# v's product of an attention layer by nested seven-product multiplication, with the softmax denominators moved and a new range test

## The chip, the cores and the metric

One NeuronCore of one Trainium2 chip runs the whole program. The metric is the device time of one execution in microseconds. All numbers are float32.

## The reference

Two layers on x of 8 images, 512 channels, 32 x 32 = 1024 positions. The first is attention with 8 heads of 64 channels and a residual, the second a "non-local" block, followed by a normalization over images and positions, channel by channel:

```python
q = conv1x1(x, Wq, bq).reshape(B, h, d, n)      # likewise k, v;  h = 8, d = 64, n = 1024
attn = softmax(einsum('bhdn,bhdm->bhnm', q, k) * d ** -0.5, axis=-1)
out = einsum('bhnm,bhdm->bhdn', attn, v).reshape(B, C, H, W)
x = x + conv1x1(out, Wp, bp)
...
g_x, theta_x, phi_x = (conv1x1(x, w, b).reshape(b, 256, n) for each)
f = einsum('bcn,bdn->bcd', theta_x, phi_x) / n
z = conv1x1(einsum('bcd,bdn->bcn', f, g_x), W_w, W_b) + x
out = (z - mean(z)) * rsqrt(var(z) + 1e-5) * gamma + beta   # over images and positions
```

## The kernel before

`attention_nonlocal_kernel` (L23) runs `unshifted`, which takes exp of the scores without subtracting a maximum. At its end a number comes back that says whether this was safe; if not, `shifted` computes all of it again in the usual way. In the profile of this kernel no instruction of `shifted` stands.

**The stages of an image.** The loop of L859 goes over the images b. For each it issues, in this order: the attention of image b (L436), then q, v and k of image b+1 (L890, L897, L910), then the output projection of image b (`project`, L595), theta and phi (`theta_phi`, L612), and g, f, Wf and z (`nonlocal_`, L679). Image 0's q, k and v come ahead of the loop (L844 to L857). The last image has its own variant; the final normalization is `last_z` (L803).

**Seven products.** A product of two matrices cut into 2 x 2 blocks needs eight block products; `seven` (L263) does it with seven, on sums of blocks that were made beforehand (`weight_sums`, `data_sums`: "t1" to "t4" of x). Each product is accumulated in a PSUM slot of 128 x 1024 (two banks). Four such slots exist, their tags in the list `free`; each stage takes them in that list's order and puts the list in a new order, `next_bank` takes the first and puts it last. A finished product is read out by ScalarE where it is the first to reach its part of the output (`first`), by VectorE where it is added (`add`).

**Nested products.** For q and k (and Wp in images 1 to 6) three (two) of the seven products are replaced by seven smaller ones each, on blocks of 128 x 128: `INNER` (L115) says which, `inner_blocks` and `inner_parts` name the smaller blocks, `keep_inner` (L163) makes the weight sums once and keeps them in DRAM, and `nested` (L245) is a generator that yields after each small product. `STEPS` and `READS` (L241, L242) write by hand after which "unit" of the outer products a small product is issued and an outer slot is read; there are 16 units, and `fills` hangs further work on a unit. v (`values`, L408) isn't nested: it runs all of `SEVEN` with the positions on the output's partitions, so data are the weights that TensorE loads and the moving operand is 256 columns of WvT (L290).

**Attention.** A step makes the scores of 128 keys for 512 queries of two heads (L462, four tiles of 64 x 64 side by side), exp on ScalarE (L465), a running sum `acc` on VectorE (L471), and the product with v (L488). After eight steps `spread` (L503) folds the 128 x 1024 sum to 32 partitions by DMAs that add (`together`, L498: one on SP, three on GpSimd's queue, one behind the other). After every fourth unit a second such fold halves it again into `t[:, 2]` (L522). `all_denominators` (L526) sums the rest over partitions by matmul with `folds8` (`columns`, L431: two tiles of 128 x 64), takes reciprocals (L534), writes them to DRAM (L536), and `rows_of` (L553) spreads them over partitions by four DMAs from SP. `normalize` (L560) gives one function that multiplies o by them, four instructions of 128 x 1024 (L571). Both are hung on products of v: the denominators behind product 1, the multiplications behind product 5 (L897). `r` and the folded sums share one buffer.

**The test.** `heads_of` (L377) takes the peak of |q| and |k| of each channel (L397, four reductions each). `bound_scores` (L421) bounds all scores by the sum over a head of their products (one small matmul, L425), writes one gate per pair of heads, and GpSimd multiplies q by the gate (L429). The minimum of all gates is the result (L968 to L973). `bound_scores` stands within `theta_phi` for images 1 to 7 (L942) and within v for image 0 (L856).

**What sets the order.** Instructions given to `pe`, `dve` or `sp` (L62) keep the order of the program on their engine. The others are placed by a planner that may move them ahead. Every load is a DMA from SP unless said otherwise; weights lie in two buffers, so a load starts when the stage before last has let go of its buffer (`load_w`, L124).

Of the kernel before, what the change touches and what calls it, by code (L numbers as in the profile page):

```python
# [16 lines left out]
P = 128  # L17
HEADS = 8
EPS = 1e-5
BOUND = 60.0  # L20
# [10 lines left out]
def unshifted(ctx: ExitStack, tc: tile.TileContext, a: dict, out: bass.AP):  # L31
# [83 lines left out]
    INNER = {"WqT": (1, 2, 6), "WkT": (1, 2, 6), "WpT": (1, 2)}  # L115
# [26 lines left out]
    def weights(name, sums_done=False):  # L142

        n, w = loaded.pop(0)
        assert n == name
        if name not in kept:
            if not sums_done:
                weight_sums(w, corner[name])
            if name not in ("WqT", "WkT"):
                keep("plain" if name == "WpT" else name, w)  # L150
        return w
# [11 lines left out]
    def keep_inner(name, w):  # L163

        for n in range(len(INNER[name])):
            a11, a12, a22, a21, s2, s3, s4 = inner_blocks(w, name, n)
            for to, l, r, op in ((s3, a11, a21, ALU.subtract), (a21, a21, a22, ALU.add), (s2, a21, a11, ALU.subtract),
                                 (s4, a12, s2, ALU.subtract)):
                nc.vector.tensor_tensor(to, l, r, op)
        wide = len(INNER[name]) * 3 * P  # L170
        kept[name] = dram.tile([P, 14 * w.shape[3] + wide], F32, tag=f"kept_{name}", name=f"kept_{name}")
        nc.sync.dma_start(kept[name][:, :14 * w.shape[3]], w.rearrange("p i k f -> p (i k f)"))
        nc.sync.dma_start(kept[name][:, 14 * w.shape[3]:], rest[name][:, :wide])
# [71 lines left out]
    def nested(name, stage, w, data, tags, first, add):  # L245
# [3 lines left out]
        for n, (q, di, begins) in enumerate(goes_to[i] for i in INNER[stage]):  # L249
# [3 lines left out]
            for _, wi, di, s, reads in SEVEN:  # L253
                ps = pair[s % 2 if s < 2 else 1][:, s // 2, n % 2 * 256:(n % 2 + 1) * 256]
                pe(nc.tensor.matmul(ps, a[wi], d[di], start=s not in begun, stop=True, skip_group_check=True))  # L255
                begun.add(s)
                for to, is_first in reads:
                    c = rows(q).start + int(to[0]) - 1
                    at = cols(q).start + (int(to[1]) - 1) * 256
                    (first if is_first and begins else add)((slice(c, c + 1), slice(at, at + 256)), ps)  # L260
                yield

    def seven(name, w, data, positions_out, first, add, between=None, early=False,  # L263
# [10 lines left out]
        if inner:  # L274
            free[:] = [tags[1], tags[2], tags[3], tags[0]]
            steps = nested(name, inner, w, data, tags[2:], first, add)
# [6 lines left out]
        for n, m in HALVES if three else ((n, None) for n in range(len(products))):  # L283
# [12 lines left out]
            work = [(*part, k) for part in (parts if m is None else parts[m:m + 1]) for k in range(nk)]  # L296
            if by_chunk and what in ("11", "s1t1"):
                work.sort(key=lambda one: one[4])
            for to_ps, at, lhsT, rhs, k in work:
                pe(nc.tensor.matmul(to_ps, lhsT(k), rhs(k), start=(s, at) not in begun, stop=(k == nk - 1),  # L300
                                    skip_group_check=True))
                begun.add((s, at))
                for ahead in (True, False):
# [25 lines left out]
    heads = const.tile([P, P], F32, tag="heads", name="heads")  # L329
    nc.vector.memset(heads, 0.0)  # L330
# [13 lines left out]
    for i in range(WARM):  # L344
        pe(nc.tensor.matmul(ps[:, :P], heads, heads, start=True, stop=True))
# [10 lines left out]
    for i in range(4):  # L356
        nc.vector.memset(folds[i * P // 4:(i + 1) * P // 4, i * D // 4:(i + 1) * D // 4], 1.0)
    folds8 = const.tile([P, D], F32, tag="folds8", name="folds8")
    nc.gpsimd.memset(folds8, 0.0)
    nc.gpsimd.affine_select(out=folds8, in_=folds8, compare_op=ALU.is_gt, fill=1.0, base=1 - P // 8,  # L360
                            pattern=[[-P // 8, 8], [0, D // 8]], channel_multiplier=1)
    nc.gpsimd.affine_select(out=folds8, in_=folds8, compare_op=ALU.is_ge, fill=0.0, base=0,
                            pattern=[[-P // 8, 8], [0, D // 8]], channel_multiplier=1)
    for j in range(2):
        nc.vector.memset(heads[j * D:(j + 1) * D, j * D:(j + 1) * D], 1.0)
    mv = const.tile([P, CC, 2], F32, tag="mv", name="mv")
    gates = const.tile([P, B * NPAIR], F32, tag="gates", name="gates")
# [9 lines left out]
    def heads_of(b, what, w, bias, data, pin=lambda ins: None, later=None, **how):  # L377

        t = mats.tile([P, CC, N], F32, tag=what, name=f"{what}_{b}")
        peak = small.tile([P, CC], F32, tag=f"peak_{what}", name=f"peak_{what}_{b}")  # L380
# [15 lines left out]
        def peak_of(c):  # L396
            ins = nc.vector.tensor_reduce(peak[:, c:c + 1], t[:, c, :], AX.X, ALU.max, apply_absolute_value=True)  # L397
            if b == 0 or later is not None:
                dve(ins)

        for c in range(CC):
            if later is None:
                peak_of(c)
            else:
                later.append(lambda c=c: peak_of(c))
        return t, peak

    def values(b, w, data, between=None):  # L408
        v = mats.tile([P, NB, C], F32, tag="v", name=f"v_{b}")

        def at(q):
            return v[:, (int(q[1]) - 1) * NB // 2:int(q[1]) * NB // 2, (int(q[0]) - 1) * C // 2:int(q[0]) * C // 2]

        def as_v(ps):
            return ps.rearrange("p h (i f) -> p (h i) f", f=C // 2)

        seven(f"pv_{b}", w, data, True, lambda q, ps: nc.scalar.copy(at(q), as_v(ps)),  # L417
              lambda q, ps: dve(nc.vector.tensor_tensor(at(q), at(q), as_v(ps), ALU.add)), between)
        return v

    def bound_scores(b, q, k, peak_q, peak_k):  # L421

        nc.vector.tensor_tensor(peak_q, peak_q, peak_k, ALU.mult)
        ps = next_bank(f"bound_{b}")[:, 0, :]
        pe(nc.tensor.matmul(ps[:, :CC], heads, peak_q, start=True, stop=True))  # L425
        gate = gates[:, b * NPAIR:(b + 1) * NPAIR]
        nc.vector.tensor_scalar(gate, ps[:, :CC], BOUND / SCALE, 1.0, ALU.is_le, ALU.mult)  # L427
        for p in range(NPAIR):
            nc.gpsimd.tensor_scalar(q[:, p, :], q[:, p, :], gate[:, p:p + 1], 1.0, ALU.mult, ALU.mult)  # L429
# [6 lines left out]
    def attention(b, q, k, v, near_end, make_f=None):  # L436
# [66 lines left out]
        def spread(u, pin=lambda ins: None, meanwhile=lambda: None):  # L503
# [18 lines left out]
            if i == 3 and not make_f:  # L522
                two = t[:, g, :].rearrange("(r s) n -> s r n", s=2)
                together(t[g * D:(g + 1) * D, 2, :], [two[0], two[1]])

        def all_denominators(ps):  # L526
# [4 lines left out]
            t, ps = t[:, 2, :], ps[:, 0, :]  # L531
            columns(ps, folds8, lambda j: t[:, j * 512:(j + 1) * 512])
            ri = t[:, :512]
            nc.vector.reciprocal(ri, ps)  # L534
            d = dram2.tile([16, 512], F32, tag="den", name=f"den_d_{b}")
            nc.sync.dma_start(d, ri.rearrange("(a s) n -> a s n", a=16)[:, 0, :])  # L536
            d = d.rearrange("(j g i) n -> g j (i n)", j=2, g=2)
            return d[0], d[1]

        def denominators(g, ps):  # L540
# [8 lines left out]
            d = dram2.tile([8, 512], F32, tag=f"den{g}", name=f"den_d_{b}_{g}")  # L549
            nc.sync.dma_start(d, ri.rearrange("(a s) n -> a s n", a=8)[:, 0, :])  # L550
            return d.rearrange("(j i) n -> j (i n)", j=2)

        def rows_of(g, d):  # L553
# [3 lines left out]
            for j in range(2):  # L557
                sp(nc.sync.dma_start(rows[g][j * D:(j + 1) * D, :], d[j].partition_broadcast(D)))

        def normalize(d):  # L560
# [6 lines left out]
            def products():  # L567
                for g in range(2):
                    for h in range(NH):
                        at = o["o"][:, 2 * g:2 * g + 2, h * 512:(h + 1) * 512]  # L570
                        dve(nc.vector.tensor_tensor(at, at, r[:, 4 * g + h:4 * g + 4:2, :], ALU.mult))  # L571

            return products
# [179 lines left out]
    late, z = {}, {}  # L753
# [90 lines left out]
    q, peak_q = heads_of(0, "q", weights("WqT", True), bq, data, early=True, by_chunk=True)  # L844
    keep_inner("WqT", w_first)
    load_w(nc.sync)
# [5 lines left out]
    w = weights("WkT")  # L852
    k, peak_k = heads_of(0, "k", w, bk, data)
    keep_inner("WkT", w)
    load_w(nc.sync)
    v = values(0, weights("WvT"), data, {3: lambda: bound_scores(0, q, k, peak_q, peak_k)})  # L856
    load_w(nc.sync)  # L857
    held = {}
    for b in range(B):  # L859
# [23 lines left out]
        if not last:  # L883
            later, of_22, of_t4 = [], [], []
# [4 lines left out]
                     8: lambda: (of_22[0](), of_22[1]()), 9: lambda: (of_22[2](), of_22[3]())}  # L889
            q, peak_q = heads_of(b + 1, "q", weights("WqT"), bq, nxt["data"], dve, inner="WqT",  # L890
                                 later=later, fills=fills)
            load_w(nc.sync)

            def norm():
                nxt["products"] = normalize(denominators(next_bank(f"den_{b}")))

            v = values(b + 1, weights("WvT"), nxt["data"], {1: norm, 2: lambda: [one() for one in later], 5: lambda: nxt["products"]()})  # L897
# [7 lines left out]
            else:  # L905
                w_p = loaded[1][1]
                for unit, which in ((12, (3, 4)), (14, (5, 6))):
                    fills[unit] = lambda which=which: weight_sums(w_p, corner["WpT"], which, dve)
            later_k = []
            k, peak_k = heads_of(b + 1, "k", weights("WkT"), bk, nxt["data"], later=later_k, inner="WkT",  # L910
                                 fills=fills)
# [3 lines left out]
        else:  # L915
# [4 lines left out]
            normalize(nxt["d"])()  # L920
# [16 lines left out]
        elif b > B - LATE and b != B - 2:  # L937
# [3 lines left out]
                       {5: lambda: b < B - 2 and of_theta.append(f_sums(b, tps[0], 0)), 1: lambda: [one() for one in later_k[:2]], 2: lambda: [one() for one in later_k[2:]],  # L941
                        4: lambda: bound_scores(b + 1, q, k, peak_q, peak_k)})  # L942
# [20 lines left out]

    last_z()


    good = const.tile([P, 1], F32, tag="good", name="good")
    nc.vector.tensor_reduce(good, gates, AX.X, ALU.min)  # L968
# [215 lines left out]
```

## Time and profile before

| what | us |
|---|---|
| median of 3 runs | 2145.33 |
| lowest and highest run | 2145.25, 2148.92 |
| span of the profiled execution, first to last instruction | 2143.6 |
| median less that span | 1.7 |

The profiled execution has no other time of its own than the span; the 1.7 us stand for what lies around the instructions. The granted TensorE clock was 0.996 of full speed in the mean.

Where the span goes, for the attention of image 1 and what follows it, by the first TensorE instruction of each stage on the timeline:

| stage | from | to | us |
|---|---|---|---|
| attention of image 1 | 343.48 | 453.51 | 110.03 |
| q of image 2 | 453.51 | 476.42 | 22.91 |
| v of image 2, with the denominators of image 1 | 476.42 | 501.80 | 25.38 |
| k of image 2 | 501.80 | 524.60 | 22.80 |
| projection of image 1 | 524.60 | 547.80 | 23.20 |
| theta and phi | 547.80 | 572.20 | 24.40 |

How to read the lines: a matmul of float32 stands as two PE rows. The duration of a row holds the way through the array, so two rows overlap; what a row costs TensorE is the distance between starts. A row of the timeline joins like instructions: start, length, engine, line, operation, output and inputs, "128*128" the part of the array, the shape of the moving operand and the count.

### The profile page before, as it was taken

How to read it: one execution, taken by the hardware profiler on the slowest of the kernel's cores; microseconds unless marked ns; L12 is line 12 of the kernel's file. 1: busy time of each engine (PE TensorE's matmuls, PEld its weight loads, DVE VectorE, ACT ScalarE, POOL GpSimd, SP SyncE). 2: the span in 40 equal slices, each digit the busy share in tenths (PEclk: the TensorE clock that was granted, in tenths of full speed). 3: DMA queues.
4: the chain of work that ended last, by engine and by line, in shares of the span. 5: the costliest groups of instructions: out<-in, count | busy, mean ns of one | idle time of the engine just before them, and what ended most of it. 6: DMA issues, size and time to landing. Idle time of an engine off the chain costs nothing.

```text
span 2143.6 us, 30444 instructions
## 1 busy us (share of the span) xinstructions
PE 2119.6 (99%) x12654; PEld 1123.3 (52%) x12654; DVE 1448.4 (68%) x1795; ACT 742.8 (35%) x848; POOL 193.2 (9%) x242
## 2 busy tenths in 40 slices
PE   9999999999999999999999999999999999999996
PEld 4534664356733567335673366633666347743462
DVE  6467667667676676766667667676675676756736
ACT  1464104641046310463105621066212652056106
POOL 0111000110001100011001100011000110011000
PEclk9999999999999999999999999999999999999998
DMA  6433443334143331433323342233434235122758
GB/s 242 137 46 58 136 166 127 49 71 129 73 131 49 79 116 73 133 50 83 109 102 109 48 100 99 97 107 50 108 132 161 42 45 139 52 60 39 227 197 341
DMA packets 53969, 231.05 MB, mean 108 GB/s; under 512 B 9792, under 2 KB 16192, under 8 KB 46272
## 3 DMA queue, kind: packets, MB, share of 16 engines
q1 hardware_dynamic: 42144, 199.26, 27.5%
q0 software_dynamic: 10192, 28.46, 11.0%
q8 instruction: 101, 1.65, 0.3%
q10 hardware_dynamic: 1488, 1.32, 0.2%
q14 instruction: 44, 0.36, 0.1%
HBM read 141.84 MB, written 46.27 MB: 88 GB/s over the span
## 4 chain that ended last, share of the span: by engine, by line
PE 96%; ACT 1%; DVE 1%; DMA 1%; issue 0%; SPq 0%; ACTq 0%; DVEq 0%
PE ps L462 21%; PE po L488 21%; PE pv L300 9%; PE ptp L300 9%; PE pp L300 7%; PE pk L300 6%; PE pq L300 5%; PE pg L300 4%; PE pk_in_s L255 3%; PE pq_in_s L255 3%; PE pz L300 2%; PE pf L658 2%; PE pp_in_s L255 2%; PE pwf L713 1%; ACT z L830 1%; PE pf L674 1%
## 5 line engine op out<-in xcount | busy, mean ns | idle before, releaser
L465 ACT ACTIVATE e<-ps 128x1024 f32<-128x1024 f32 x512 | 522.6, 1024 | 431.1 <-PE ps L462 425.6
L471 DVE TENSOR_TENSOR acc<-acc,e 128x1024 f32<-128x1024 f32 x384 | 470.0, 1224 | 143.7 <-ACT e L465 140.3
L462 PE MATMUL ps<-q,k 64*64 64x512 f32 x4096 | 529.4, 589 | 0.0
L488 PE MATMUL po<-e,v 64*64 64x512 f32 x4096 | 528.7, 589 | 0.0
L488 PEld LDWEIGHTS po<-e,v 64*64 64x64 f32 x4096 | 156.6, 133 | 282.9 <-issue 275.4
L462 PEld LDWEIGHTS ps<-q,k 64*64 64x64 f32 x4096 | 155.5, 133 | 283.8 <-issue 274.8
L501 POOL DMA_DIRECT2D fold<-acc x189 | 147.1, 779 | 978.9 <-DMA fold<-acc 576.6
L701 ACT ACTIVATE g<-pg,gb 128x512 f32<-128x512 f32 x31 | 21.3, 687 | 475.4 <-PE pg L300 475.3
L469 DVE TENSOR_TENSOR acc<-e,e 128x1024 f32<-128x1024 f32 x64 | 78.3, 1224 | 136.6 <-ACT e L465 136.6
L300 PE MATMUL pv<-w_WvT,t_x 128*128 128x256 f32 x512 | 116.4, 381 | 0.0
L300 PE MATMUL ptp<-w_tp,t_x 128*128 128x256 f32 x512 | 114.4, 379 | 0.0
L417 ACT COPY v<-pv 128x1024 f32<-128x1024 f32 x32 | 32.4, 1012 | 213.9 <-PE pv L300 213.9
L300 PEld LDWEIGHTS pv<-w_WvT,t_x 128*128 128x128 f32 x512 | 96.6, 190 | 18.5 <-issue 5.7
L300 PEld LDWEIGHTS ptp<-w_tp,t_x 128*128 128x128 f32 x512 | 97.3, 190 | 13.2
L300 PE MATMUL pq<-t_x,w_WqT 128*128 128x512 f32 x200 | 100.1, 592 | 0.8 <-DVE t_x L842 0.8
L300 PE MATMUL pp<-t_o,w_WpT 128*128 128x512 f32 x208 | 100.8, 592 | 0.0
L300 PE MATMUL pk<-t_x,w_WkT 128*128 128x512 f32 x200 | 100.0, 592 | 0.0
L429 POOL TENSOR_SCALAR q<-q,gates 128x1024 f32<-128x1024 f32 x32 | 35.1, 1109 | 718.4 <-DVE gates L427 718.4
L300 PE MATMUL ptp<-w_tp,x 128*128 128x256 f32 x384 | 87.4, 381 | 0.0
L300 PE MATMUL pv<-w_WvT,x 128*128 128x256 f32 x384 | 86.8, 379 | 0.0
L324 DVE TENSOR_TENSOR q<-q,pq_in_s 128x256 f32<-128x256 f32 x119 | 48.6, 420 | 51.1 <-PE pq_in_s L255 38.4
L324 DVE TENSOR_TENSOR k<-k,pk_in_s 128x256 f32<-128x256 f32 x119 | 47.9, 420 | 48.6 <-PE pk_in_s L255 36.0
(195 smaller groups left out, 2348.6 us busy)
## 6 DMA issues: line engine op xcount, KB each, us to landing
fold<-acc POOLq DMA_DIRECT2D x189, 128.0 KB, 3.1
w_WqT<-kept_WqT SPq DMA_DIRECT2D x7, 2368.0 KB, 8.8
w_WkT<-kept_WkT SPq DMA_DIRECT2D x7, 2368.0 KB, 8.8
r<-den_d SPq DMA_DIRECT2D x32, 512.0 KB, 6.9
x<-in_x_dram SPq DMA_DIRECT2D x30, 512.0 KB, 5.7
w_WpT<-kept_WpT SPq DMA_DIRECT2D x6, 2176.0 KB, 8.3
w_WvT<-kept_WvT SPq DMA_DIRECT2D x7, 1792.0 KB, 7.2
w_tp<-kept_tp SPq DMA_DIRECT2D x7, 1792.0 KB, 7.3
```

The lines of the kernel that those rows point to most:

```text
L255: pe(nc.tensor.matmul(ps, a[wi], d[di], start=s not in begun, stop=True, skip_group_check=True))
L300: pe(nc.tensor.matmul(to_ps, lhsT(k), rhs(k), start=(s, at) not in begun, stop=(k == nk - 1), skip_group_check=True))
L324: pin(nc.vector.tensor_tensor(at, at, ps if len(ps.shape) == 3 else ps.unsqueeze(1), ALU.add))
L417: seven(f"pv_{b}", w, data, True, lambda q, ps: nc.scalar.copy(at(q), as_v(ps)), lambda q, ps: dve(nc.vector.tensor_tensor(at(q), at(q), a ...
L429: nc.gpsimd.tensor_scalar(q[:, p, :], q[:, p, :], gate[:, p:p + 1], 1.0, ALU.mult, ALU.mult)
L462: pe(nc.tensor.matmul(ps[c * P // 2:(c + 1) * P // 2, j, :], k[r, p, keys], q[r, p, h * 512:(h + 1) * 512], start=True, stop=True, skip_gr ...
L465: nc.scalar.activation(e, ps, AF.Exp, scale=SCALE)
L469: nc.vector.tensor_tensor(accs[u], es[u, 0], e, ALU.add)
L471: ins = nc.vector.tensor_tensor(accs[u], accs[u], e, ALU.add)
L488: pe(nc.tensor.matmul(ps[j * D:(j + 1) * D, r, :], v[keys, m, (2 * p + j) * D:(2 * p + j + 1) * D], e[keys, j, :], start=(m == 0), stop=(m ...
L501: nc.gpsimd.dma_start(to, part_of, accum_op=ALU.add)
L658: pe(nc.tensor.matmul(to, theta[l][:, i, :], phi[r][:, i, :], start=(i == 0), stop=(i == NB // 2 - 1), skip_group_check=True))
```

## The change

It is made in `unshifted` only.

- **v is nested like q and k.** `INNER` gets WvT with the same three products; `nested` and `seven` learn the case `positions_out`, in which a small product is two matmuls of 128 moving columns; v's outer products are the four of `FOUR`. Between q and v the list `free` is put in another order by hand.
- **The denominators come at unit 14 of q**, into the slot `free[0]`. The second fold is gone; the matmul uses four tiles of 32 columns (`folds4`), and the reciprocals are of 128 x 256. The order of the reciprocals in DRAM is another, and `rows_of` and `product` address them accordingly. The reciprocal is pinned.
- **The multiplications are hung one by one** on units 10 to 13 of v.
- **The test is another**: peaks, `bound_scores` and gates are gone; the reciprocals of all denominators are loaded back at the end (`own`, nine DMAs) and each has to lie between 1e-20 and 1e20.
- **Around image 0**: q's and k's additions and WkT's sums are pinned, `keep_inner("WqT")` moves behind WkT's sums and is pinned, `keep_inner("WvT")` stands behind v.

```diff
-    INNER = {"WqT": (1, 2, 6), "WkT": (1, 2, 6), "WpT": (1, 2)}
+    INNER = {"WqT": (1, 2, 6), "WkT": (1, 2, 6), "WvT": (1, 2, 6), "WpT": (1, 2)}
...
-                nc.vector.tensor_tensor(to, l, r, op)
+                dve(nc.vector.tensor_tensor(to, l, r, op))
...
-                pe(nc.tensor.matmul(ps, a[wi], d[di], start=s not in begun, stop=True, skip_group_check=True))
+                if positions_out:
+                    ps = ps.rearrange("p (i f) -> p i f", f=P)
+                    for i in range(2):
+                        pe(nc.tensor.matmul(ps[:, i, :], d[di][:, i * P:(i + 1) * P], a[wi], start=s not in begun and not i,
+                                            stop=True, skip_group_check=True))
+                else:
+                    pe(nc.tensor.matmul(ps, a[wi], d[di], start=s not in begun, stop=True, skip_group_check=True))
                 begun.add(s)
                 for to, is_first in reads:
+                    if positions_out:
+                        (first if is_first and begins else add)((q, int(to[0]) - 1, int(to[1]) - 1), ps)
+                        continue
...
-            work = [(*part, k) for part in (parts if m is None else parts[m:m + 1]) for k in range(nk)]
+            each = len(parts) // 2
+            work = [(*part, k) for part in (parts if m is None else parts[m * each:(m + 1) * each]) for k in range(nk)]
...
+                if three and positions_out and not i % 2:
+                    continue
...
-        def peak_of(c):
-            ins = nc.vector.tensor_reduce(peak[:, c:c + 1], t[:, c, :], AX.X, ALU.max, apply_absolute_value=True)
...
-    def bound_scores(b, q, k, peak_q, peak_k):
...
-            if i == 3 and not make_f:
-                two = t[:, g, :].rearrange("(r s) n -> s r n", s=2)
-                together(t[g * D:(g + 1) * D, 2, :], [two[0], two[1]])
...
-            t, ps = t[:, 2, :], ps[:, 0, :]
-            columns(ps, folds8, lambda j: t[:, j * 512:(j + 1) * 512])
-            ri = t[:, :512]
-            nc.vector.reciprocal(ri, ps)
...
+            ps, of = ps[:, 0, :256], P // 4
+            for g in range(2):
+                for i in range(4):
+                    pe(nc.tensor.matmul(ps[i * of:(i + 1) * of, :], folds4[:, g * of:(g + 1) * of],
+                                        t[:, g, i * 256:(i + 1) * 256], start=(g == 0), stop=(g == 1),
+                                        skip_group_check=True))
+            ri = t[:, 2, :256]
+            dve(nc.vector.reciprocal(ri, ps))
+            d = dram.tile([of, 256], F32, tag=f"den{b}", name=f"den_d_{b}")
+            nc.sync.dma_start(d, ri.rearrange("(x s) n -> x s n", s=4)[:, 0, :])
+            own.append((dens[:, b * 64:(b + 1) * 64], d.rearrange("x (y n) -> (x y) n", y=4)))
+            return d.rearrange("(j h g i) m -> g j h i m", j=2, h=2, g=2)
...
-            def products():
-                for g in range(2):
-                    for h in range(NH):
-                        at = o["o"][:, 2 * g:2 * g + 2, h * 512:(h + 1) * 512]
-                        dve(nc.vector.tensor_tensor(at, at, r[:, 4 * g + h:4 * g + 4:2, :], ALU.mult))
-
-            return products
+            def product(g, h):
+                at = o["o"][:, 2 * g:2 * g + 2, h * 512:(h + 1) * 512]
+                of = r[:, 4 * g + h:4 * g + 4:2, :]
+                if not make_f:
+                    of = r[:, 4 * g:4 * g + 4, :].rearrange("q (k a) (c m) -> q (a c) k m", k=2, c=2)[:, h::2]
+                    at = at.rearrange("q p (k m) -> q p k m", k=2)
+                dve(nc.vector.tensor_tensor(at, at, of, ALU.mult))
+
+            return [lambda g=g, h=h: product(g, h) for g in range(2) for h in range(NH)]
...
-    q, peak_q = heads_of(0, "q", weights("WqT", True), bq, data, early=True, by_chunk=True)
-    keep_inner("WqT", w_first)
-    load_w(nc.sync)
+    q = heads_of(0, "q", weights("WqT", True), bq, data, dve, early=True, by_chunk=True)
...
-    w = weights("WkT")
-    k, peak_k = heads_of(0, "k", w, bk, data)
+    w = weights("WkT", pin=dve)
+    keep_inner("WqT", w_first)
+    load_w(nc.sync)
+    k = heads_of(0, "k", w, bk, data, dve)
     keep_inner("WkT", w)
     load_w(nc.sync)
-    v = values(0, weights("WvT"), data, {3: lambda: bound_scores(0, q, k, peak_q, peak_k)})
+    w = weights("WvT")
+    v = values(0, w, data)
+    keep_inner("WvT", w)
...
+                     14: lambda: nxt.update(products=normalize(denominators(bank(free[0], f"den_{b}"))))}
+            q = heads_of(b + 1, "q", weights("WqT"), bq, nxt["data"], dve, inner="WqT", fills=fills)
             load_w(nc.sync)
...
-            v = values(b + 1, weights("WvT"), nxt["data"], {1: norm, 2: lambda: [one() for one in later], 5: lambda: nxt["products"]()})
+            free[:] = [free[2], free[1], free[0], free[3]]
+            v = values(b + 1, weights("WvT"), nxt["data"], inner="WvT",
+                       fills={unit: lambda i=i: nxt["products"][i]() for i, unit in enumerate((10, 11, 12, 13))})
...
-                        4: lambda: bound_scores(b + 1, q, k, peak_q, peak_k)})
+                       {5: lambda: b < B - 2 and of_theta.append(f_sums(b, tps[0], 0))})
...
+    for to, d in own:
+        nc.sync.dma_start(to, d)
     last_z()
...
-    nc.vector.tensor_reduce(good, gates, AX.X, ALU.min)
+    nc.vector.tensor_scalar(sane, dens, 1.0 / SANE, 1.0, ALU.is_ge, ALU.mult)
+    nc.vector.scalar_tensor_tensor(sane, dens, SANE, sane, ALU.is_le, ALU.mult)
+    nc.vector.tensor_reduce(good, sane, AX.X, ALU.min)
```

## The prediction

> **What bounds the kernel now.** I read the page first: which engine is busy, and what the chain that ended last is made of.
>
> ```profile
> PE 2119.6 (99%) x12654; PEld 1123.3 (52%) x12654; DVE 1448.4 (68%) x1795; ACT 742.8 (35%) x848; POOL 193.2 (9%) x242
> PE 96%; ACT 1%; DVE 1%; DMA 1%; issue 0%; SPq 0%; ACTq 0%; DVEq 0%
> ```
>
> TensorE (PE) is never idle for long, and the chain is TensorE nearly throughout. A busy PE can still be a slow PE, so next I read the timeline of one steady image row by row, to see whether rows follow each other at a constant pace.
>
> ```profile
> 317.81 1.05 PE L658 MATMUL pf<-tp 128*128 128x128 f32 x8
> 318.70 1.06 PE L658 MATMUL pf<-s_phi,s_theta 128*128 128x128 f32 x8
> ...
> 324.06 1.88 PE L300 MATMUL pg<-x,w_WgT 128*128 128x512 f32 x4
> ...
> 476.42 3.62 PE L300 MATMUL pv<-w_WvT,x 128*128 128x256 f32 x16
> 479.87 3.62 PE L300 MATMUL pv<-w_WvT,t_x 128*128 128x256 f32 x16
> 483.42 1.08 PE L434 MATMUL den<-fold,folds 128*64 128x512 f32 x4
> 484.43 3.72 PE L300 MATMUL pv<-w_WvT,t_x 128*128 128x256 f32 x16
> ...
> 501.80 3.60 PE L300 MATMUL pk<-x,w_WkT 128*128 128x512 f32 x8
> 505.23 0.59 PE L255 MATMUL pk_in_s<-x,w_WkT 128*128 128x256 f32 x2
> ```
>
> From start to start: 8 rows of 512 columns take 505.23 - 501.80 = 3.43 us, 0.429 each; 16 rows of 256 take 479.87 - 476.42 = 3.45, 0.216 each; the 56 rows of 128 of the product f take 324.06 - 317.81 = 6.25, 0.1116 each. A row costs its columns and little else. k of image 2 is 32 rows of 512 and 42 of 256: 13.73 + 9.07 = 22.80 us, exactly what the stage takes (501.80 to 524.60). So the nested stages run without a gap although VectorE (DVE) reads every small product behind them. The time of this kernel is its count of columns plus a few stalls, and I price the change that way.
>
> **The nested v, seven images.** Before: 7 products of 8 matmuls, 112 rows of 256, 112 x 0.2159 = 24.18 us. After: four outer products, 64 rows of 256, 13.82 us; and 3 x 7 small products of two matmuls, 84 rows of 128, 84 x 0.1116 = 9.37 us. Together 23.19: 0.99 us less an image, 7.0 us in seven. The price of a 128-column row decides: it breaks even at (24.18 - 13.82) / 84 = 0.1234 us. The nearest row is f's, with the same 128 x 128 weights, loaded anew for every matmul. Below it lies half a 256-column row, 0.108 (2.2 us more gain); above, the mean 0.190 of a weight load in the rows of PEld, which would be the pace if loads were not hidden (46 us lost). I take 0.1116, since f shows them hidden.
>
> The Trainium skill speaks against this part: "TensorE: Matmul & The Clock Gate", section "Back-to-back issue gap", says that a stream of pairs of weight load and matmul sustains about 81 ns at 128 columns and 131 ns at 512, so that a short matmul is dear per column. By that ratio a row of 128 would be an estimated 0.429 x 81 / 131 = 0.265 us, and the nested v would lose 83 us in all. This case's rows stand at 0.1116 against 0.429, a ratio of 0.26 where the page has 0.62; I go by the rows.
>
> Does VectorE keep up in v? Of the 21 small reads four go to ScalarE, 17 to VectorE at 0.42; with three outer reads and four multiplications of 1.22 that is 15.7 us in 23.2. In q's window before it is 15.62 busy in 22.91, without a gap on TensorE. If this cover were gone, a late read stops TensorE at the next small product that accumulates into the same slot; that is the second rival. The reductions of the peaks (eight an image, 1.16 to 1.22 each) and GpSimd's gating (35 us in all) go, but hid behind TensorE: worth nothing.
>
> **The denominators.** They cost TensorE four rows of 512 in two tiles, two at a time, plus the way in and out of that tiling: from where the next v row was due (483.11 + 0.22 = 483.33) to 484.43, and 0.1 more behind, 1.2 us. After: 16 rows of 256 in four tiles of 32 columns, that is four rounds of 0.216 = 0.86 if four run side by side as the 64 x 64 tiles of attention do (eight rows of 512 in 0.86), plus the same way in and out (0.34): 1.2 again. No row shows 128 x 32 tiles. Ends: 0.86 (gain 0.34 an image) and one after the other, 16 x 0.216 + 0.34 = 3.8 (loss 2.6). I take 1.2, by the attention row. The skill's page "TensorEngine Tiling (Array Packing)", section "Available Configurations", lists 128 x 32 as four tiles; no run here shows it, and by it the sum is the one I take.
>
> They now come some 8 us earlier than before, so what they wait for matters:
>
> ```profile
> 468.36 0.51 SPq L499 DMA_DIRECT2D fold<-fold  x1
> 487.93 0.50 SPq L536 DMA_DIRECT2D den_d<-fold  x1
> 489.85 2.40 SPq L558 DMA_DIRECT2D r<-den_d  x4
> 473.37 1.22 DVE L324 TENSOR_TENSOR q<-q,pq 128x1024 f32<-128x1024 f32 x1
> 476.96 2.34 DVE L324 TENSOR_TENSOR q<-q,pq 128x1024 f32<-128x1024 f32 x2
> 484.55 3.36 DVE L534 RECIPROCAL fold<-den 128x512 f32<-128x512 f32 x1 [5.25 <-PE den L434]
> 502.35 2.36 DVE L571 TENSOR_TENSOR o<-o,r 128x1024 f32<-128x1024 f32 x2 [0.31 <-DMA r<-den_d]
> ```
>
> The first fold is complete when SP issues the second, at 468.36. Behind unit 14's small product the new matmul is due at 475.13: 6.8 us to spare. The second fold, whose last part GpSimd issued at 472.84 and which lands 3.1 later by the median, would have been too late; it is gone. Its slot is that of the outer product whose last read is the VectorE row at 473.37, done at 474.6: 0.5 to spare. The reciprocal, at 3.36 us for 512 columns, is 1.7 for 256, pinned ahead of q's last three reads: it waits until 476.4 and ends at 478.1, and those reads end at 480.8 instead of 479.3. v starts at 477.5 and needs the slot they read only in its unit 4, at 482. Then SP: store, spreading from 480.0, the fourth DMA issued at 481.8, landed by its median of 6.9 us at 488.7 (longest 11.5: 493.3). Unit 10 of v, where the first multiplication is due, ends at 477.5 + 11 x 0.864 + 14 x 0.446 = 493.2. k's weights, which SP issued at 476.61, wait behind the spreading until 482.4 and land about 9 us later; k starts at 500.7. All covered; cost nothing.
>
> **The bound's matmul goes, eight times.** theta and phi are 112 rows, 24.18 us, and the stage takes 572.20 - 547.80 = 24.40: 0.22. For image 0 v takes 78.30 - 53.80 = 24.50: 0.32. Sum 7 x 0.22 + 0.32 = 1.8 us.
>
> **The start.** TensorE loses 1.0 us at 15.96, waiting for a sum of x:
>
> ```profile
> 13.79 0.29 DVE L169 TENSOR_TENSOR w_WkT<-w_WkT 128x128 f32<-128x128 f32 x1 [1.86 <-DMA w_WkT<-in_WkT_dram]
> 14.00 0.69 DVE L842 TENSOR_TENSOR w_WqT<-w_WqT 128x512 f32<-128x512 f32 x1
> 14.60 1.22 DVE L842 TENSOR_TENSOR t_x<-x,t_x 128x1024 f32<-128x1024 f32 x1
> 15.96 3.67 PE L300 MATMUL pq<-t_x,w_WqT 128*128 128x512 f32 x8 [0.84 <-DVE t_x L842]
> ```
>
> A sum of `keep_inner` that nobody needs yet stands ahead of it on VectorE and waits 1.86 us for WkT. Pinned behind q's additions it can't. The last piece of x, issued at 7.97, lands by the median of 5.7 at 13.7, so the sum could start 0.9 earlier. Nothing later in image 0 shows a gap that would eat it. I take 0.9, between 0 and 1.0.
>
> **Around image 0 and at the end.** `keep_inner("WvT")` adds 12 sums of 0.29 to the start of attention, where VectorE is busy 77.78 of 110.03 us: hidden, 3.5 us if not. The test adds nine loads on an idle SP and three VectorE instructions of 128 x 512, about 0.5 + 0.7 + 0.6. The old minimum ran as soon as its inputs were there (1869), not at the end, so I take 0; in the last VectorE chain it would be 1.8.
>
> **Sum.** -7.0 - 1.8 - 0.9 = -9.7 us on the span of 2143.6: 2133.9. The median run is 1.7 above that span; I keep this distance: 2145.33 - 9.7 = **2135.6 us**.
>
> **Rivals.**
> *Slower: the four 32-column tiles run one after the other.* Then 7 x 2.6 = 18.2 comes back: 2153.8. It decides from 2.6 us a call (1.2 + 9.7 / 7). For it: no such row in the trace, and each pair of rows of one matmul meets the same tile. Against: 64-column and 64 x 64 tiles do overlap.
> *About the same: VectorE is late in v.* In units 10 to 13 it gets four multiplications, one outer addition and seven small reads. Back to back, rows follow at 1.13 (two rows in 2.34) and 0.34 (by the same overlap of 0.085): 5 x 1.13 + 7 x 0.34 = 8.0 us, where TensorE takes 4 x 0.864 + 7 x 0.446 = 6.6. It ends 1.4 behind, and a small product two further on in the same slot comes 1.3 later. If 1 us of it reaches TensorE in each image, 7.0 comes back: 2142.6. For it: k, the model, has only two such operations in a row; and a multiplication already waited 0.31 for `r`. Against: VectorE enters unit 10 without arrears, and `r` has 4.5 us to spare by the median, none by the longest.
> *The change doesn't do what it says: rows of 128 are dear here*, because each is aimed at another piece of PSUM, where f stays on one for four matmuls, and the loads show. At 0.190 a row, 84 x 0.078 x 7 = 46 comes back: 2181.6. Against: q's and k's small products change their piece as often and cost their columns.
>
> **Chances.** Forecast 0.76; late VectorE 0.13; serial tiles 0.08; dear rows 0.03. 0.2% of the time is 4.3 us, about what a measurement of this kernel tells from no change: faster 0.77 (a mild lateness of VectorE counts here), same 0.12, slower 0.11. The forecast's own range is 2133 to 2139 (cheaper rows and denominators below; start, test and WvT's sums above). The range reaches to the late VectorE: 2133 to 2143.5, and leaves out the two slower cases.
>
> **What would show it.** v's stage at 23.2 us without a gap, its rows of 128 at 0.11; a den group in q at unit 14 that takes 1.2 in four rounds, with no wait ahead of it; theta and phi at 24.18; the wait at 15.96 gone; a multiplication that doesn't wait for `r`. Wrong would be: gaps at v's small products, den rows that start 0.2 apart, or a VectorE test in the last 20 us.

## The result and the profile after

The changed kernel takes 2152.64 us in the median of 7 runs (2151.52 to 2154.09), the kernel before 2145.59 in 7 (2145.25 to 2148.92). The ratio is 1.0031, 95% interval 1.0021 to 1.0042: slower by 7.05 us. That lies above the range of the prediction. The profiled execution of the changed kernel has a span of 2152.2 us, 8.6 more than before. It is the slowest of the seven (2154.09, 1.45 above the median), so its trace shows a little more loss than the median has; the last section shows a loss of 1.45 us that one execution may have and another not.

The page of the changed kernel, its engines and its chain of waits:

```profile
PE 2116.7 (98%) x12974; PEld 1124.5 (52%) x12974; DVE 1412.1 (66%) x1855; ACT 745.9 (35%) x869; POOL 144.9 (7%) x193
PE 89%; DMA 6%; DVE 2%; ACT 1%; issue 1%; SPq 1%; DVEq 0%; ACTq 0%
```

TensorE has fewer us of work than before (2119.6) in a longer span, and its share of the chain fell from 96% to 89%: DMA took 6% of it, where it had 1%. So the question is not what TensorE does more slowly, but which transfer it waits for. The chain itself answers; it is read in order of time around the end of q and v of image 2 (start, length, what):

```profile
476.03 1.04 PE den L523 x16
...
477.10 1.76 DVE fold L527
...
478.97 9.17 DMA den_d<-fold
...
490.26 10.48 DMA r<-den_d
...
501.98 1.22 DVE v L420
...
503.77 0.71 PE pv_in_s L258 x4
```

The denominators (`den`, 16 rows of TensorE), the reciprocal (`fold`, L527), its store to DRAM (`den_d`), the spreading of it over partitions (`r`), a row of VectorE and then the last small product of v: the path of the reciprocals, which the prediction held to be covered, sets the end. Its first transfer, 32 KB, takes 9.17 us. SP's own queue at that time shows what stands ahead of it:

```profile
478.55 0.33 SPq L134 DMA_DIRECT2D w_WkT<-kept_WkT  x1
478.97 0.49 SPq L529 DMA_DIRECT2D den_d<-fold  x1
488.28 2.59 SPq L555 DMA_DIRECT2D r<-den_d  x4
```

k's weights (2368 KB) were issued 0.4 us ahead of the store. The spreading needs the store landed, so it begins at 488.28, 9.3 us behind the store. This image is the worst: in the other six the distance is 8.2 to 8.4. In the kernel before it was 1.9 us (487.93 to 489.85), since there the weights were issued 11 us ahead of the store:

```profile
476.61 0.33 SPq L134 DMA_DIRECT2D w_WkT<-kept_WkT  x1
487.93 0.50 SPq L536 DMA_DIRECT2D den_d<-fold  x1
```

VectorE and then TensorE at the end of v in the changed kernel:

```profile
493.86 0.42 DVE L420 TENSOR_TENSOR v<-v,pv_in_s 128x256 f32<-128x256 f32 x1 [0.89 <-PE pv_in_s L258]
496.12 1.23 DVE L572 TENSOR_TENSOR o<-o,r 128x1024 f32<-128x1024 f32 x1 [1.84 <-DMA r<-den_d]
497.26 0.75 DVE L420 TENSOR_TENSOR v<-v,pv_in_s 128x256 f32<-128x256 f32 x2
...
500.84 1.23 DVE L572 TENSOR_TENSOR o<-o,r 128x1024 f32<-128x1024 f32 x1 [0.84 <-DMA r<-den_d]
501.98 1.21 DVE L420 TENSOR_TENSOR v<-v,pv 128x1024 f32<-128x1024 f32 x1
503.30 0.42 DVE L420 TENSOR_TENSOR v<-v,pv_in_s 128x256 f32<-128x256 f32 x1
```

```profile
495.86 1.03 PE L310 MATMUL pv<-w_WvT,t_x 128*128 128x256 f32 x4
497.73 0.71 PE L258 MATMUL pv_in_s<-w_WvT,i_x 128*128 128x128 f32 x4 [0.84 <-DVE v L420]
...
501.39 1.03 PE L310 MATMUL pv<-w_WvT,t_x 128*128 128x256 f32 x4
503.77 0.71 PE L258 MATMUL pv_in_s<-w_WvT,i_x 128*128 128x128 f32 x4 [1.36 <-DVE v L420]
504.32 3.60 PE L310 MATMUL pk<-x,w_WkT 128*128 128x512 f32 x8
```

In these rows VectorE keeps to the program's order. Its first multiplication of `o` waits 1.84 us for `r`, the third 0.84, and v's small reads (`v<-v,pv_in_s`, the additions that empty a small product's slot) queue behind them. TensorE's next small product accumulates into a slot that such a read has yet to empty. After the four rows at 495.86 it was due at 496.73 and starts at 497.73; after those at 501.39 it was due at 502.25 and starts at 503.77. That is 2.5 us of the 2.77 by which v of this image (25.96 us) exceeds the 23.19 that its columns alone cost.

The spans by stage, before and after, from the starts of their first matmuls, account for the 8.6 us:

| stages | before | after | difference |
|---|---|---|---|
| q, denominators and v, images 1 to 7 | 339.2 | 347.9 | +8.7 |
| k, images 1 to 7 | 159.9 | 162.1 | +2.2 |
| theta and phi with the bound | 195.1 | 193.5 | -1.6 |
| v of image 0 | 24.5 | 24.3 | -0.2 |
| start up to k of image 0 | 29.8 | 29.9 | +0.1 |
| the rest (projection and tail) | | | -0.6 |

The nested v itself takes 178.0 us in the seven images; its columns are 7 x 23.19 = 162.3. So 15.7 us of v are stops, and they are what turned a gain into a loss. Of the +2.2 in k, 1.45 stand in image 5 alone, where the granted clock fell for a while (last section).

### The profile page after: what moved, and what is told of

Its sections match the earlier page's. It is cut to its first block, busy times and chain, and to the rows that moved or that the text cites. A ratio compares the mean times of both kernels' runs of the same rounds, so it can differ in the third digit from the quotient of the medians.

```text
span 2152.2 us, 31116 instructions
## 1 busy us (share of the span) xinstructions
PE 2116.7 (98%) x12974; PEld 1124.5 (52%) x12974; DVE 1412.1 (66%) x1855; ACT 745.9 (35%) x869; POOL 144.9 (7%) x193
## 4 chain that ended last, share of the span: by engine, by line
PE 89%; DMA 6%; DVE 2%; ACT 1%; issue 1%; SPq 1%; DVEq 0%; ACTq 0%
PE ps L454 20%; PE po L480 20%; PE ptp L310 9%; PE pp L310 7%; PE pk L310 5%; PE pq L310 5%; PE pg L310 4%; DMA r<-den_d 3%; PE pk_in_s L261 3%; PE pq_in_s L261 3%; DMA den_d<-fold 3%; PE pz L310 2%; PE pf L659 2%; PE pp_in_s L261 2%; PE pwf L714 1%; PE pv L310 1%
## 5 line engine op out<-in xcount | busy, mean ns | idle before, releaser
L310 PE MATMUL pv<-w_WvT,t_x 128*128 128x256 f32 x400 | 100.7, 380 | 0.0
L420 DVE TENSOR_TENSOR v<-v,pv_in_s 128x256 f32<-128x256 f32 x119 | 48.5, 420 | 62.5 <-PE pv_in_s L258 48.5
L310 PEld LDWEIGHTS ptp<-w_tp,x 128*128 128x128 f32 x384 | 73.0, 190 | 13.3 <-issue 3.8
L310 PEld LDWEIGHTS pv<-w_WvT,t_x 128*128 128x128 f32 x400 | 69.6, 191 | 6.0
L400 ACT ACTIVATE k<-pk,bk 128x512 f32<-128x512 f32 x50 | 31.6, 683 | 114.8 <-PE pk L310 114.8
```

The costliest lines, as they stand in the source:

```text
L400: nc.scalar.activation(t[:, c, cols(q)], ps[:, m, :], AF.Identity, bias=bias[:, c:c + 1])
```

## The experiments

The theory: the order on SP's queue. The store stands behind the weights, `r` comes late, and VectorE's queue carries the lateness to TensorE. The main rival: VectorE simply has too much to do at the end of v, whatever `r` does. Another: the nested v is dear in itself. The first four kernels ran on one chip beside a kernel before of 2145.98 us (29 runs), the last three on another beside one of 2145.81 (15 runs). All ratios are to the kernel before.

**weights_behind.** The load of k's weights is pinned on SP (given to `sp`), so that it keeps its place in the program: behind the store and the four spreading DMAs.

```diff
-    def load_w(dma):
+    def load_w(dma, pin=lambda ins: None):
...
             ins = dma.dma_start(t[:, :of.shape[1]], of)
+            pin(ins)
...
             q = heads_of(b + 1, "q", weights("WqT"), bq, nxt["data"], dve, inner="WqT", fills=fills)
-            load_w(nc.sync)
+            load_w(nc.sync, sp)
```

> The changed kernel with one DMA moved: the load of k's weights is pinned on SP behind the four DMAs that spread the reciprocals. Theory A (the 2.4 MB load stands ahead of the store of the reciprocals on SP; r comes some 7 us late, VectorE waits for it with v's small reads behind, TensorE stops): the store lands in about 2 us, no multiplication waits for r, v takes 23.2 us in each image instead of 24.6 to 26.4, 2136 us in all (2145.6 - 9.2). Theory B (VectorE has too much to do in units 10 to 13 of v even with r in time): v stays at 24.2 or more, 2143 us. Theory C (small products of 128 columns are slow by themselves): no change, 2152 us.

2139.18 us, ratio 0.9971 (0.996 to 0.9982). v takes 23.58 in each of the seven images, k 22.86 from image 2 on. SP's queue, and then VectorE:

```profile
476.68 0.49 SPq L530 DMA_DIRECT2D den_d<-fold  x1
478.57 2.59 SPq L556 DMA_DIRECT2D r<-den_d  x4
481.26 0.58 SPq L134 DMA_DIRECT2D w_WkT<-kept_WkT  x1
```

```profile
495.40 0.94 DVE L421 TENSOR_TENSOR v<-v,pv_in_s 128x256 f32<-128x256 f32 x2
496.25 1.22 DVE L573 TENSOR_TENSOR o<-o,r 128x1024 f32<-128x1024 f32 x1
497.39 1.21 DVE L421 TENSOR_TENSOR v<-v,pv 128x1024 f32<-128x1024 f32 x1
498.71 0.42 DVE L421 TENSOR_TENSOR v<-v,pv_in_s 128x256 f32<-128x256 f32 x1
499.04 1.22 DVE L573 TENSOR_TENSOR o<-o,r 128x1024 f32<-128x1024 f32 x1
```

The spreading begins 1.9 us after the store's issue, no multiplication of this image waits for `r`, and k doesn't wait for its weights, though they are issued 4.6 us behind the store and land 16 us after that. This one edit takes the ratio from 1.0031 to 0.9971, some 13 us. That the weights go ahead of the store is the cause of the loss. It is still 3 us more than theory A expected (2136). What stays is a small remainder of the rival: VectorE's rows follow one another without a wait and still the small read at 498.71 is late. TensorE loses 0.39 us an image by it (23.58 against 23.19).

**other_queue.** The weights stay where they are, and the store and the spreading are issued from GpSimd's queue instead of SP's.

```diff
-            nc.sync.dma_start(d, ri.rearrange("(x s) n -> x s n", s=4)[:, 0, :])
+            nc.gpsimd.dma_start(d, ri.rearrange("(x s) n -> x s n", s=4)[:, 0, :])
...
-                    sp(nc.sync.dma_start(to, d[j].rearrange("h i m -> h (i m)").partition_broadcast(D)))
+                    sp(nc.gpsimd.dma_start(to, d[j].rearrange("h i m -> h (i m)").partition_broadcast(D)))
```

> The changed kernel, with the store of the reciprocals and their spreading issued by GpSimd's queue; k's weights are still loaded from SP just ahead. If the store is late because it stands in SP's own line behind the weights: it lands in about 2 to 3 us as the folds do from that queue (3.1 by the median), r is in time, about 2137 us. If it is late because the DMA engines are full with the weights whatever the queue: it lands after 7 to 9 us as before, 2151 to 2153 us. Theory C: 2152 us either way.

2142.42 us, ratio 0.9983 (0.9974 to 0.9993). v takes 23.58 to 25.20. GpSimd's queue:

```profile
480.13 0.58 POOL L529 DMA_DIRECT2D den_d<-fold  x1 [12.02 <-DVE q L336]
487.11 2.34 POOL L555 DMA_DIRECT2D r<-den_d  x4 [6.40 <-PE pv_in_s L258]
```

Neither of the two expected times came; the result lies between them. The spreading begins 7.0 us behind the store in this image and 6.9 to 7.3 in images 3 to 7, where the changed kernel has 8.2 to 8.4: another queue takes off some 1.2 us, not the 6.4 that would bring it to 1.9. GpSimd's wait is put down to a matmul, but what ends it is the store: SP's own load of the same reciprocals, which waits for it too, starts at 486.42, 6.3 us after the store's issue, and GpSimd's first spreading DMA follows 0.7 later. The weights that SP had issued at 479.52 are still under way. So what the store stands behind is mostly the transfer, and not SP's queue alone. The Trainium skill says why in "DMA: Bandwidth & Descriptors", section "Issuing engines are not separate DMA queues": DMAs from all issuing engines run on the same 16 DMA engines and interleave. The 6.9 to 7.3 here agree with it.

**products_in_k.** The order on SP is as in the changed kernel, but nothing in v waits for `r`: the four multiplications are hung on units 1 to 4 of k.

```diff
-            v = values(b + 1, weights("WvT"), nxt["data"], inner="WvT",
-                       fills={unit: lambda i=i: nxt["products"][i]() for i, unit in enumerate((10, 11, 12, 13))})
+            v = values(b + 1, weights("WvT"), nxt["data"], inner="WvT")
...
+            fills.update({unit: lambda i=i: nxt["products"][i]() for i, unit in enumerate((1, 2, 3, 4))})
```

> The changed kernel with the four multiplications hung on units 1 to 4 of k instead of units 10 to 13 of v; the weights are still ahead of the store. Theory A: r is as late as before, but nobody in v waits for it; v 23.2 us, k 22.8 to 23.5 (r lands about 4 us ahead of k), 2136 to 2139 us. Theory B: v 23.2 as well, but k, which has other fills, loses what v gains: 2139 to 2143. Theory C: v stays at 25, 2152 us.

2144.53 us, ratio 0.9993 (0.9984 to 1.0003): no difference to the kernel before. The stages v and k of image 2, one line each (stretch, length, then busy time and count of PE, PEld, DVE, ACT, POOL, the granted clock, DMA's share, GB/s), and k's stop:

```profile
476.56:499.75 23.19, 23.19 (x150) 21.55 (x149) 10.94 (x21) 4.52 (x7) 0.00 (x0) 1.00 0.71 199
499.75:523.72 23.97, 23.58 (x77) 13.65 (x76) 19.91 (x32) 5.64 (x10) 0.00 (x0) 1.00 0.25 93
```

```profile
506.75 0.70 PE L261 MATMUL pk_in_s<-x,w_WkT 128*128 128x256 f32 x2 [0.39 <-DVE k L336]
```

The nested v without the multiplications takes 23.19, PE busy all of it: the third theory is out, the products themselves cost what was forecast. But the time is above all that theories A and B expected (2136 to 2143), because k now takes 23.97 instead of 22.86: its own small reads queue behind the multiplications. The multiplications aren't free at these units of k either.

**v_not_nested.** Everything of the change but the nested v: seven products as before, the multiplications behind product 5.

```diff
-            v = values(b + 1, weights("WvT"), nxt["data"], inner="WvT",
-                       fills={unit: lambda i=i: nxt["products"][i]() for i, unit in enumerate((10, 11, 12, 13))})
+            v = values(b + 1, weights("WvT"), nxt["data"], between={5: lambda: [one() for one in nxt["products"]]})
```

> The changed kernel with v by seven products as before the change, the multiplications behind product 5; the denominators stay at unit 14 of q, the weights ahead of the store, the new test stays. Theory A: r lands about when product 5 ends, and few reads stand behind it; v 24.2 us without a stop; what is left of the change is the bound's matmuls, 2143 to 2144 us, so nesting v with the late r costs 9 us where it should have brought 7. Theory B: the same. Theory C: the same, so this run measures nesting alone and tells only how much of the loss is v's.

2143.76 us, ratio 0.9987 (0.9978 to 0.9997). SP's queue and the stage v:

```profile
477.15 0.33 SPq L134 DMA_DIRECT2D w_WkT<-kept_WkT  x1
477.57 0.49 SPq L529 DMA_DIRECT2D den_d<-fold  x1
485.88 2.59 SPq L555 DMA_DIRECT2D r<-den_d  x4
```

```profile
476.95:501.12 24.17, 24.17 (x113) 21.29 (x112) 8.72 (x9) 3.04 (x3) 0.00 (x0) 1.00 0.68 190
```

The spreading begins 8.3 us behind the store here too, and it costs nothing: v takes exactly its 24.17, PE busy throughout. The four multiplications follow product 5's read, at 499.01 on VectorE, and don't wait: by then `r` has landed. That is 22.1 us into v; in the changed kernel the first was due at 494.3, 15.9 us into v, and waited. VectorE is busy for only 8.72 us of this stage. So the loss is made by two parts of the change together, the late store and the early use of `r` in the nested v. Neither the order on SP nor the nested v has such a price alone.

**half_ahead.** A dose: the first half of k's weights goes ahead of the store as before, the second half behind the spreading.

```diff
+            if ahead:
+                at = of.shape[1] // ahead
+                dma.dma_start(t[:, :at], of[:, :at])
+                with tc.issue_after(spread_last[-1]):
+                    dma.dma_start(t[:, at:of.shape[1]], of[:, at:])
+                return
...
-            load_w(nc.sync)
+            load_w(nc.sync, 2)
```

> The changed kernel with k's weights loaded in two halves: the first still ahead of the store of the reciprocals on SP, the second behind the spreading. Theory A (the bytes ahead of the store set its delay): the store lands after about 5 us instead of 9, r some 4 us earlier than in the changed kernel and 3 later than with all weights behind, the first multiplication waits for nothing or little; v 23.6 to 24.2 us, 2139 to 2143 us. If any load ahead does the harm (a queue that changes over, not bytes): 9 us again, 2152.

2140.01 us, ratio 0.9973 (0.9961 to 0.9984).

```profile
476.21 0.33 SPq L136 DMA_DIRECT2D w_WkT<-kept_WkT  x1
476.63 0.49 SPq L535 DMA_DIRECT2D den_d<-fold  x1
482.02 2.59 SPq L561 DMA_DIRECT2D r<-den_d  x4
484.65 0.60 SPq L138 DMA_DIRECT2D w_WkT<-kept_WkT  x1
```

The spreading follows the store by 5.4 us here. Over the seven images it is 1.8 to 1.9 with nothing ahead, 5.2 to 5.6 with 1.2 MB, 8.2 to 9.3 with 2.4 MB. Half the bytes make about half the delay, so bytes set it and not a load as such. These 3.5 us of lateness are just about the slack: v takes 23.58 in six images, as with the weights behind, but 24.22 in the last, where the third multiplication waits 0.54 us for `r`. With the 5 to 6 us of other_queue v takes 23.98 in the mean.

**behind_units_8_11.** weights_behind, and the multiplications two units earlier, where VectorE has less to do.

```diff
-                       fills={unit: lambda i=i: nxt["products"][i]() for i, unit in enumerate((10, 11, 12, 13))})
+                       fills={unit: lambda i=i: nxt["products"][i]() for i, unit in enumerate((8, 9, 10, 11))})
```

> The weights behind the spreading, and the four multiplications on units 8 to 11 of v instead of 10 to 13, so that unit 13, with its outer addition, holds none. The 0.39 us that v still takes over its columns (23.58 against 23.19) is by theory VectorE's arrears at unit 13. If so: v 23.2 us, 2136 to 2137 us. If the multiplications themselves are what is too much wherever they stand in v: 23.6 again, 2139. r lands about 13 us into v, when unit 10 runs; if that is too late for the third multiplication (unit 10), a short wait shows there.

2136.78 us (2136.35 to 2136.97), ratio 0.9958 (0.9945 to 0.9972): the fastest of all, 9.0 us below the kernel before. Stages v and k:

```profile
476.12:499.31 23.19, 23.19 (x150) 21.54 (x148) 15.23 (x25) 4.52 (x7) 0.00 (x0) 1.00 0.70 199
499.31:522.17 22.86, 22.86 (x76) 13.98 (x75) 15.62 (x28) 5.64 (x10) 0.00 (x0) 1.00 0.26 98
```

Both stages are now nothing but columns. Two of the multiplications of this image wait for `r` (0.84 and 0.35 us on VectorE), which costs TensorE nothing: VectorE has slack at that place, as v's 23.19 shows. So the 0.39 of weights_behind was VectorE's arrears at the end of v.

**behind_three_and_one.** weights_behind, with only the fourth multiplication moved away, to unit 2 of k. It tests whether the arrears are made by the multiplication at unit 13 itself.

```diff
-                       fills={unit: lambda i=i: nxt["products"][i]() for i, unit in enumerate((10, 11, 12, 13))})
+                       fills={unit: lambda i=i: nxt["products"][i]() for i, unit in enumerate((10, 11, 12))})
...
+            fills[2] = nxt["products"][3]
```

> The weights behind the spreading, three multiplications on units 10 to 12 of v and the fourth on unit 2 of k. By the same theory v takes 23.2 us, and k, which has one operation of 1.22 us more at a unit without other work, 22.8 to 23.1: 2136 to 2138 us. If it is the number of operations and not the place: 2138 to 2139.

2139.51 us, ratio 0.997 (0.996 to 0.9981), and v still takes 23.58: a miss. The late read comes ahead of the fourth multiplication, as the rows of weights_behind show (498.71 against 499.04). The arrears come from the multiplications at units 10 to 12 and the outer addition at 497.39. Moving the last one helps nothing; moving all of them forward does.

## Why the prediction was wrong, point by point

**The step that failed** is the one on the queue: "k's weights, which SP issued at 476.61, wait behind the spreading until 482.4". With it stands the term that was put at nothing ("All covered; cost nothing"). The weights went ahead of the store. The prediction followed the order of the program's text, in which the load stands behind the denominators. But neither that load nor the store is pinned, so the planner's order holds. In the trace the load is ready when q lets go of its weight buffer (q ends at 478.36), the store half a microsecond later, when the reciprocal is done (478.86). Whether the planner went by this is not shown. In the kernel before the same load also went first, but 11 us ahead of the store, and had landed. The prediction moved the store to the one place where a transfer of 2.4 MB starts, named both, and assumed their order. In place of the store landing at once (1.8 us in the kernel before), it took 8.1 to 9.2, and the spreading began 8.9 to 9.9 us into v instead of 2.4 with the weights behind. Price: 13.0 of the 15.7 us of stops in v, that is all but the 7 x 0.39 that stay with `r` in time, and perhaps the 1.45 us in k of image 5, where the clock fell behind a stop.

**The spreading's length** was misread as well, and that hid how little there was to spare. "Landed by its median of 6.9 us at 488.7" gives the fourth DMA of an image the median of all 32. But the later ones of the four take longer: in the kernel before, in image 2, the second took 6.7 us from issue to landing, the third 9.6, the fourth 10.6. By that the fourth would have landed at 492.4, 0.8 us ahead of the unit's end at 493.2 and not 4.5. The range's "longest" covered it. In the changed kernel it took 10.48 (490.26 to 500.74), no more than before: it was late by its issue. The weights behind the spreading land 16 us after their issue in weights_behind, not 9; that cost nothing, since k starts some 2 us later still.

**Late VectorE in v** was a rival, with the right place ("units 10 to 13") and the right mechanism. Its size was put at 1 us an image; with `r` in time it is 0.39, 2.7 us in seven. In the changed kernel the late `r` comes on top of these arrears, in the same queue.

**The nested v** was priced rightly: 23.19 us forecast, 23.19 measured wherever nothing stops it (products_in_k, behind_units_8_11). The rows of 128 columns cost 0.1116 as f's rows do, so "dear rows" is out, and with it the estimate by issue gaps that would have lost 83 us.

**The denominators** were priced rightly: the same cost in q as before in v. q with them takes 24.11 where it took 22.91, 1.20 more. The 16 rows in tiles of 32 columns stand in one line of the changed kernel:

```profile
475.96 1.07 PE L523 MATMUL den<-fold,folds 128*32 128x256 f32 x16
476.96 1.13 PE L310 MATMUL pq<-t_x,w_WqT 128*128 128x512 f32 x2
```

Sixteen rows of 256 columns in 1.00 us are four rounds of 0.25: four run side by side, and "serial tiles" is out.

**The bound's matmuls**: theta and phi take 24.17 instead of 24.40, v of image 0 24.26 instead of 24.50. Forecast 1.8 in all (its own terms, 7 x 0.22 + 0.32, make 1.9), measured 1.6 + 0.2.

**The start**: the wait at 15.96 is gone, yet k of image 0 starts at 29.90 instead of 29.77. The trace shows where the gain of about 1 us went: the first three rows of q, from 4.64 on, start 0.85, 0.85 and 0.81 us apart instead of 0.43, which loses 1.2. Its record of the full granted clock begins only at 7.10 us, that of the kernel before at 4.54. In the seven experiments, whose program up to there is that of the changed kernel, it begins between 4.33 and 6.27, and rows ahead of it are slow in the same way. k of image 0 starts at 28.54 where it begins first (products_in_k), at 28.90 where it begins at 4.80, nearest to the kernel before (half_ahead), and at 30.60 where it begins at 6.27 (other_queue, which also waits 0.83 us at 9.06). So the 0.9 was there, and one execution's late clock hid it. This is read from the traces; no run tests it.

**The cover around image 0, the range test, the reductions and the gating**: nothing was forecast and nothing is seen. The test's three instructions run at 2096.7 to 2098.6, where VectorE waits for TensorE next, and the tail after the last theta and phi is 0.4 us shorter than before.

What the forecast's sum was worth is seen where nothing stops v. behind_units_8_11 has a span of 2134.5 against 2143.6: 9.1 us less, where 9.7 were forecast. By stages, rounded, that is -7.0 for q, denominators and v together, -1.8 for the bound's matmuls, -0.4 at the start, -0.7 for projection and tail, and +0.7 in k.

## What to carry to other kernels

When a small transfer on the path to a result is moved, look at which large transfers become ready within a few microseconds of it, and fix the order by hand. Here two unpinned DMAs became ready half a microsecond apart, and the trace of the kernel before, where 11 us lay between them, couldn't show what their nearness would cost. A wait on an engine that keeps to its order costs what is queued behind it: a store that took over 8 us cost nothing in a v that used `r` 6 us later, and some 1.9 us an image (13.0 in seven) in the nested one. When a chain of like DMAs sets a time, take the landing of its last one and not the median of all. And hang the instructions that may wait where the engine has slack, ahead of its busiest stretch and not within it.

## What the runs showed of the hardware

A 32 KB store behind a 2.4 MB load in the same queue took 8.2 to 9.3 us until the next dependent issue, behind 1.2 MB 5.2 to 5.6, with a free line 1.8 to 1.9, and from GpSimd's queue beside the 2.4 MB 6.9 to 8.0.

In image 5 of the changed kernel the clock fell behind a stop. The rows of TensorE, and the windows behind the stop (columns as above):

```profile
1293.94 1.03 PE L310 MATMUL pv<-w_WvT,t_x 128*128 128x256 f32 x4
1297.05 0.99 PE L258 MATMUL pv_in_s<-w_WvT,i_x 128*128 128x128 f32 x4 [2.08 <-DVE v L420]
1297.83 5.05 PE L310 MATMUL pk<-x,w_WkT 128*128 128x512 f32 x8
1302.72 0.59 PE L261 MATMUL pk_in_s<-x,w_WkT 128*128 128x256 f32 x2
```

```profile
1297.83:1301.30 3.47, 3.47 (x6) 1.54 (x6) 3.23 (x5) 0.00 (x0) 0.00 (x0) 0.58 0.68 211
1301.30:1322.14 20.84, 20.84 (x70) 13.03 (x69) 12.95 (x25) 5.65 (x10) 0.00 (x0) 1.00 0.17 72
```

TensorE was due at 1294.81 and started at 1297.05, 2.24 us late (idle for 2.08 by the profile). Then the granted clock was 0.58 in the mean of the next 3.5 us (0.50 from 1297.34 on, for 3.41 us), and eight rows of 512 took 4.89 us instead of 3.43. That is 1.45 us on top of the stop; k of this image takes 24.31 instead of 22.87. This idle time is the longest of TensorE ahead of the tail in the nine traces, and this fall of the clock is their only one there; after the next longest, 1.86 us in image 4 of the same trace, the clock stayed at 1.00. The 1.45 is also what this execution has above the median of the seven; whether the others had such a fall is not on record. The Trainium skill, "TensorE: Matmul & The Clock Gate", section "Why this matters for your kernels", asks for no idle gaps of more than about 3 us. Here the fall came behind a gap of 2.08 us, so the trace is the stricter measure; one such case doesn't give a threshold, and no run tests that the gap was its cause.
